# A three-stage block on one core: column-tiled bias products, transposing DMAs for integers and a written order in the first stage

## Chip, core and metric

The kernel runs on one core of a Trainium2 chip. Its time is the device time in microseconds (us), from launch to end. A core has TensorE (PE, matrix products from SBUF into PSUM), VectorE (DVE), ScalarE (ACT), GpSimd (POOL) and SyncE (SP), which here only issues DMAs. Each engine runs its own list of instructions in order, and the engines wait for each other through semaphores. PSUM has eight banks of 128 x 512 f32.

## The reference

Two batches of 2048 tokens with 512 channels, x, go through

```
c = clip(x * styles) @ W_cond.T, scaled per channel, plus a bias      # "cond"
h = rms_norm(c) ; r, i, f, g = h @ four matrices                       # "rec"
hs = scan(a(r), sqrt(1 - a*a) * sigmoid(i) * f) * gelu(g) + c
h2 = rms_norm(hs) ; x2 = x + hs + (gelu(h2 @ Wg) * (h2 @ Wf)) @ Wo     # "up", "down"
n  = norm(x2)
b  = norm(n * pw_g[id] + pw_b[id]) * cp_g[c] + cp_b[c]                 # the branch
cat = [w0*b, w1*(n*tm_g[c] + tm_b[c]), w2*(x2+vm), w3*(x2+vn), w4*(x2+vr), w5*(n*ms_g[m] + ms_b[m])]
o  = norm(silu(cat @ int_W1 + b1) @ int_W2 + b2)
out = x2 + int8(o) @ int8(rhs) * scales
```

vm, vn and vr are vectors per batch; c and m are small classes (5 and 3), id is one of 500. int8 rounds each token by its own largest value to the range -127 to 127.

## The kernel before, in words

Tokens lie on the free axis, channels on partitions, until the last stage. All large products are f32 and are done by a scheme of seven products in place of eight: `paired` (L138) and `paired_in_place` (L174) take the four quarters of the operand and of the weight, and run seven steps, each for two halves u of the output. After given steps (`at`, `then`, keyed by step or by step and u) other pieces of work are called in. DVE makes the sums of operand quarters, POOL those of the weights (`combine`, L119).

- The first stage, `cond` (L526), runs four stretches s of 1024 tokens. ACT copies a partial product out of PSUM with scale and bias (`tap`, L559), DVE adds the rest (`put`, L580) and clips, SP stores y_d. For the norm, four squares (ACT) are added up (DVE), summed over channels on PE, and turned into an inverse root (`inv_rms`, L446), which is stored in DRAM as r_d by four DMAs on ACT's queue (`store`, L478). In the stretches s = 0 and 3 the order on PE, DVE and ACT is that of the program (`ordered`, L279); in s = 1 and 2 a scheduler chooses it.
- `recur` (L682), `up` (L744) and `down` (L858) follow. The last call of `down` also prepares the last stage: `vectors` (L1157) multiplies three state vectors with three blocks of int_W1; `vectors_and_x` (L1197) adds those blocks, and loads the second half of the weight w_int.
- The last stage takes eight blocks of 512 tokens. `by_tokens` (L1321) turns x2 to tokens on partitions by PE transposes, norms, gathers the rows of pw by POOL's indirect DMA and norms again. `by_channels` (L1371) turns norm and branch back by PE. `gains` (L1378) multiplies by the class gains: a bf16 product with one-hot rows, four row groups side by side, then a DVE multiply. `up` (L1399) is the product with w_int, its operands x2T, lnT (the norm with the ms gains), tT (with the tm gains) and hT (the branch). `down2` (L1456) is the product with int_W2. The int8 part of block i-1 runs in `up` of block i: `last_norm` after step 0, `int8_product` (L1510) after step 2, with PE transposes of the integers (L1521), a DVE eviction with the lower clip (L1523) and the product with rq (`by_rhs`, L1488). The last block has its own, finer end (`part_norm`, `part_product`).
- Ahead of block 0 the biases of the classes are multiplied with w_int (L1568 to L1591) into a table of ten rows, which POOL splits into three bf16 parts for the product at L1429. PSUM there: two tiles of two banks for transposes and gains, used in turn, and four banks for products.

Edits of the diff touch `paired_in_place`, `store`, `cond`, `vectors`, `quarters`' callers, `stats`, `rstd_of`, `gather`, `by_channels`, `gains`, `up`, `int8_product` and the code that drives the last stage (L1564 on).

## Time and profile before

| | |
|---|---|
| three timed runs, us | 2039.68, 2043.04, 2043.53 (median 2043.04) |
| the profiled execution, us | 2037.24, span 2035.5 |
| granted PE clock, mean | 0.997 |
| first stage, 0 to 117 us | PE busy 110.5 |
| rec, 117 to 504 | PE busy 387.0 |
| up, 504 to 1090 | PE busy 584.7 |
| down, 1090 to 1395 | PE busy 303.8 |
| block 0 and its biases, 1395 to 1486 | PE busy 91.0, DVE 59.1 |
| blocks 1 to 7 up to the end's start, 1486 to 1978 | PE busy 491.2, DVE 374.2 |
| the end, 1978 to 2036 | PE busy 48.0 |
| all DMA | 193.5 MB, 95 GB/s over the span |

The table gives busy time by stage. A line of the timeline has the start and length in us, the engine and source line, the operation, the output and its inputs, shapes, and a count; brackets hold the idle time ahead of it and who ended it. An f32 matmul shows as two records. "ACTq" and "SPq" are the queues in which those engines issue DMAs. A line of the waits has who waited for whom, and the total, the number of times and the longest of these waits in us.

### The profile page before, as it was taken

Reading aid. Unit: us, or ns where it says so; the run is one execution under the profiler, and the core shown is the slowest. Engines: PE = TensorE matmul, PEld = TensorE weight load, DVE = VectorE, ACT = ScalarE, POOL = GpSimd, SP = SyncE. Lnnn points to the kernel's source line nnn. Section 1 sums busy time; section 2 is a strip of 40 time slices with the busy share of each in tenths; the row PEclk is TensorE's granted clock in tenths of the full one; section 3 lists DMA queues with packets and bytes.
Section 4 is the critical chain, followed back from the end, with each engine's and each line's share of the span. In section 5 each row is a group of like instructions: output and inputs, shape, how many; then the busy total and the mean of one; then the engine's idle time right before and its main releaser. Section 6 shows DMA issues by size and latency. Waiting matters only on the chain.

```text
span 2035.5 us, 17108 instructions
## 1 busy us (share of the span) xinstructions
PE 2016.1 (99%) x6404; PEld 1073.6 (53%) x6412; DVE 1188.6 (58%) x1804; ACT 652.4 (32%) x861; POOL 155.1 (8%) x126
## 2 busy tenths in 40 slices
PE   9899999999999999999999999999999999999998
PEld 5344444444444444444444444435777777777774
DVE  6757666666534224334226375486587687688675
ACT  4457777777422222222220000001302302302301
POOL 0332000000400000000010000072000000000000
PEclk9999999999999999999999999999999999999998
DMA  6571223121412112111334765624101101111000
GB/s 214 183 215 52 83 64 96 48 93 63 152 44 92 43 42 93 42 41 64 114 117 158 259 208 199 227 88 166 54 29 63 72 33 63 65 39 62 22 21 21
DMA packets 84547, 193.54 MB, mean 95 GB/s; under 512 B 6608, under 2 KB 34806, under 8 KB 80368
## 3 DMA queue, kind: packets, MB, share of 16 engines
q1 hardware_dynamic: 79792, 175.64, 25.5%
q0 software_dynamic: 4608, 16.78, 2.5%
q8 instruction: 50, 0.82, 0.2%
q14 instruction: 33, 0.27, 0.0%
q10 hardware_dynamic: 64, 0.03, 0.0%
HBM read 133.27 MB, written 58.75 MB: 94 GB/s over the span
## 4 chain that ended last, share of the span: by engine, by line
PE 96%; DVE 2%; DMA 1%; ACT 1%; issue 0%; ACTq 0%; SPq 0%; DVEq 0%
PE up_a L132 16%; PE ps_h_a L132 11%; PE rec_a L132 11%; PE up_d L132 8%; PE dn_a L132 7%; PE ps_h_d L132 6%; PE rec_d L132 5%; PE ps_o L1467 5%; PE up_b L132 4%; PE dn_d L132 4%; PE ps_h_b L132 3%; PE rec_b L132 3%; PE y_a L132 2%; PE dn_b L132 2%; PE ps_f L1491 1%; PE y_d L132 1%
## 5 line engine op out<-in xcount | busy, mean ns | idle before, releaser
L132 PE MATMUL up_a<-h,w_up 128*128 128x512 f32 x384 | 172.6, 592 | 0.0
L132 PE MATMUL dn_a<-op,w_dn 128*128 128x512 f32 x384 | 167.4, 594 | 0.0
L773 DVE SCALAR_TENSOR_TENSOR prod<-up_d,cols,k 128x512 f32<-128x512 f32 x48 | 35.9, 750 | 201.2 <-ACT k L265 201.2
L265 ACT COPY k<-up_a 128x512 f32<-128x512 f32 x144 | 83.9, 584 | 198.2 <-PE up_a L132 194.2
L753 ACT ACTIVATE gate<-gate,cols 128x512 f32<-128x512 f32 x96 | 68.8, 721 | 215.4 <-DVE gate L752 214.3
L132 PE MATMUL up_a<-h2T,w_up 128*128 128x512 f32 x288 | 129.5, 592 | 0.0
L132 PEld LDWEIGHTS up_a<-h,w_up 128*128 128x128 f32 x384 | 73.1, 190 | 91.7 <-issue 89.3
L132 PEld LDWEIGHTS dn_a<-op,w_dn 128*128 128x128 f32 x384 | 72.3, 190 | 88.6 <-issue 86.1
L132 PE MATMUL rec_a<-h,w_rec 128*128 128x512 f32 x256 | 115.1, 592 | 0.0
L132 PE MATMUL rec_a<-hT,w_rec 128*128 128x512 f32 x256 | 115.1, 592 | 0.0
L1467 PE MATMUL ps_o<-int_w,h 128*128 128x512 f32 x224 | 103.6, 606 | 0.0
L132 PEld LDWEIGHTS up_a<-h2T,w_up 128*128 128x128 f32 x288 | 54.8, 190 | 68.8 <-issue 68.8
L132 PE MATMUL up_b<-h,w_up 128*128 128x512 f32 x192 | 86.3, 592 | 0.0
L132 PE MATMUL up_d<-h,w_up 128*128 128x512 f32 x192 | 86.3, 592 | 0.0
L132 PE MATMUL dn_d<-op,w_dn 128*128 128x512 f32 x192 | 84.2, 595 | 0.0
L132 PEld LDWEIGHTS rec_a<-h,w_rec 128*128 128x128 f32 x256 | 48.7, 190 | 61.1 <-issue 60.9
L132 PEld LDWEIGHTS rec_a<-hT,w_rec 128*128 128x128 f32 x256 | 48.7, 190 | 61.1 <-issue 60.7
L265 ACT COPY k<-rec_a 128x512 f32<-128x512 f32 x96 | 55.4, 579 | 67.3 <-PE rec_a L132 65.8
L752 DVE TENSOR_TENSOR gate<-up_b,k 128x512 f32<-128x512 f32 x48 | 32.9, 690 | 71.7 <-PE up_b L132 70.6
L132 PE MATMUL up_d<-h2T,w_up 128*128 128x512 f32 x144 | 65.2, 592 | 0.0
L1467 PEld LDWEIGHTS ps_o<-int_w,h 128*128 128x128 f32 x224 | 40.3, 190 | 46.5 <-issue 46.5
L132 PE MATMUL ps_h_a<-tT,w_int 128*128 128x256 f32 x256 | 64.3, 385 | 0.0
(394 smaller groups left out, 3474.6 us busy)
## 6 DMA issues: line engine op xcount, KB each, us to landing
pp_d<-prod SPq DMA_DIRECT2D x48, 512.0 KB
op<-pp_d SPq DMA_DIRECT2D x16, 1536.0 KB
y_d<-y SPq DMA_DIRECT2D x16, 512.0 KB
h<-y_d SPq DMA_DIRECT2D x4, 2048.0 KB
yr<-y_d SPq DMA_DIRECT2D x16, 512.0 KB
hs_d<-yr SPq DMA_DIRECT2D x16, 512.0 KB
h<-hs_d SPq DMA_DIRECT2D x4, 2048.0 KB
op<-in_xT SPq DMA_DIRECT2D x32, 256.0 KB
```

The lines of the kernel that those rows point to most:

```text
L132: ins = nc.tensor.matmul(ps, ws[k // 2][:, slot, k % 2, ts(u, P)], xs[k], start=(first and k == 0), stop=(last and k == n - 1), skip_group ...
L265: nc.scalar.copy(t, ps)
L752: nc.vector.tensor_add(gate[u][:, half], ps, kept)
L753: nc.scalar.activation(gate[u][:, half], gate[u][:, half], AF.Gelu, bias=col("L0_attn_mlp_gate_b", fs[u]),)
L773: nc.vector.scalar_tensor_tensor(prod[u][:, b_], ps, col("L0_attn_mlp_fc_b", fs[u]), kept, ALU.add, ALU.add)
L1467: nc.tensor.matmul(ps, h1[:, c, ts(j, P)], w2[:, c, :], start=(c == 0), stop=(c == C - 1))
L1491: nc.tensor.matmul(ps, qT[:, ts(c, P)], rq[:, c, :], start=(c == 0), stop=(c == C - 1))
```

## The change

Four edits come together.

1. First stage: all four stretches run in the order of the program. The operand sums of stretch s+1 are called in stretch s (the first at step 6, the second at its end, the other two at step 2 of s+1), and the squares of stretch s at steps 1 and 2 of s+1. The r_d stores of the very last inverse root go through SP.
2. `vectors` takes its twelve operands from one padded tile, filled by three copies; the loads and sums of the second half of w_int are called after step 3 of the last `down` and no longer after step 1.
3. The twelve products of the class biases are put in four column groups of 32, two accumulated and four not, and one product adds the groups up later. PE follows the program's order in the first block up to the end of step 1 of `up`; steps 0 and 1 are done in two halves of their operands each, with gains and branch transposes between. In block 0 tT holds the ms gains and lnT the tm gains, and x's second transposes are queued one half step earlier.
4. The integers are clipped on DVE ahead of the transpose, which is now a DMA on SP from SBUF to SBUF, one for each pair of 128 tokens. The product of the first pair stays behind step 2, that of the second goes behind the first half of step 3. The last block keeps its PE transposes.

```diff
     def paired_in_place(ws, B11, B21, B12, B22, banks, tap, out11, out12, out21, out22,
-                        then=(), added=None, shared=False):
+                        then=(), added=None, shared=False, late=None):
...
             X = [x[:, k, :] for x in X for k in range(x.shape[1])]
-            for u in U:
-                ins = product(ps[u], ws, slot, X, u, first and not (u and shared), last)
-                if (step.n, u) in then:
-                    then[step.n, u]()
+            if late and step.n < 2:
+                n = len(ws) // 2
+                for h in (0, 1):
+                    for u in U:
+                        ins = product(
+                            ps[u], ws[n * h : n * h + n], slot, X[2 * n * h : 2 * n * h + 2 * n], u,
+                            first and not h and not (u and shared), last and h,
+                        )
+                        if (step.n, u, h) in then:
+                            then[step.n, u, h]()
+                mids.append(ins)
+            else:
+                for u in U:
+                    ins = held["ins"] = product(
+                        ps[u], ws, slot, X, u, first and not (u and shared), last
+                    )
+                    if not u:
+                        mids.append(ins)
+                    if (step.n, u) in then:
+                        then[step.n, u]()
             ends.append(ins)
...
         step.n = 0
-        ends = []
+        ends, mids = [], []
...
         step(pa, 0, B11, True, False)
-        k1 = tap(1, pa, None)
+        with late(0) if late else nullcontext():
+            k1 = tap(1, pa, None)
         pb = banks("b")
-        sums(B11, B12, B11)
-        sums(B12, B22, B12)
-        step(pb, 1, B21, True, not added)
-        more(1, pb)
-        out11(pb, k1)
+        if late:
+            step(pb, 1, B21, True, not added)
+        with late(1) if late else nullcontext():
+            sums(B11, B12, B11)
+            sums(B12, B22, B12)
+        if not late:
+            step(pb, 1, B21, True, not added)
+        def c11():
+            more(1, pb)
+            out11(pb, k1)
+        if not late:
+            c11()
         pd = banks("d")
         step(pd, 6, B22, True, False)
+        if late:
+            c11()
         more(2, pd)
...
         out21(pa)
-        return ends
+        return ends, mids
...
+            queue = nc.sync if (m, s) == (2, NS - 1) else nc.scalar
             for j in range(4):
-                nc.scalar.dma_start(r_d[m, s][:, ts(j, n)], r[32 * j : 32 * j + 1])
+                queue.dma_start(r_d[m, s][:, ts(j, n)], r[32 * j : 32 * j + 1])
...
+    chain = {}
...
         b = s // PER_S
-        at = parts_of_rest((4, 0), *AT[1:])
+        at = merged(chain, parts_of_rest((4, 0), *AT[1:]))
         if s == 0:
...
         else:
-            xs = operands(load_x(s), f"xT_{s}")
+            xs, sums = ahead
+            at = merged(at, {(2, 1): sums[2:4]})
         y, late = {}, []
...
             ahead[:] = operand_sums(Bt, "hT_0")
-            at = merged(
-                at, {(2, 1): chunks[0:2], (3, 1): chunks[2:3], (5, 0): chunks[3:4], (6, 1): ahead[1][0:1]}
-            )
+            at = merged(at, {(2, 1): chunks[0:2], (3, 1): chunks[2:3], (5, 0): chunks[3:4]})
+        else:
+            ahead[:] = operand_sums(load_x(s + 1), f"xT_{s + 1}")
+        at = merged(at, {(6, 1): ahead[1][0:1]})
         paired([w_cond[b]], xs, f"y_{s}", tap, put(0, a_), put(0, b_), out21, put(2, b_), at)
-        if s == NS - 1:
-            ahead[1][1]()
-        tot = None
-        for o in (2, 3, 0, 1):
-            tot = squares(tot, y[o])
+        ahead[1][1]()
+        tot = []
+        def square(o):
+            tot.append(squares(tot.pop() if tot else None, y[o]))
+        chain.clear()
+        chain.update({
+            k: [lambda o=o: square(o)] for k, o in (((1, 0), 2), ((1, 1), 3), ((2, 0), 0), ((2, 1), 1))
+        })
         rest.append(inv_rms(tot, 1, s))
...
     for s in range(NS):
-        with ordered() if s in (0, NS - 1) else nullcontext():
+        with ordered():
             done = cond(s)
...
     idx_pw = w3.tile([P, NT], mybir.dt.int32, name="idx_pw", bufs=1)
-    betas = w3.tile([P, 3, C, R], FP, name="betas", bufs=1)
+    betas_flat = w3.tile([P, 3 * C * R + G - R], FP, name="betas", bufs=1)
+    betas = betas_flat[:, : 3 * C * R].rearrange("p (m c r) -> p m c r", c=C, r=R)
     dn = ph1.enter_context(ExitStack())
...
             for c in range(C):
-                lhsT = small.tile([P, G], FP, tag="vec", name=f"vec_{m}_{c}", bufs=4)
-                nc.vector.memset(lhsT, 0.0)
-                nc.vector.tensor_copy(lhsT[:, 8:10], vs[m][:, c, :])
                 nc.tensor.matmul(
-                    ps[G * c : G * c + G], lhsT, rhs(c), start=(m == 0), stop=(m == 2)
+                    ps[G * c : G * c + G], held["vec"][:, m, c, :], rhs(c),
+                    start=(m == 0), stop=(m == 2),
                 )
...
     def raw(k):
-        w = w8(f"int_w1_{k}")
-        nc.sync.dma_start(w, block_of(k))
+        w = w14(f"int_w1_{k}")
+        nc.sync.dma_start(w[:, 0:C], block_of(k))
         scaled(k, lambda c: w[:, c, :])
...
+    def vectors_as_operands(w):
+        v = padded(w, 3 * C).rearrange("p (m c) g -> p m c g", c=C)
+        for m in range(3):
+            nc.vector.tensor_copy(v[:, m, :, 8:10], vs[m])
+        held["vec"] = v
     w3_4 = [raw(3), raw(4)]
+    vectors_as_operands(w3_4[0])
     w_int, of_x = quarters(2, 1)
...
+    def second_weight():
         ws, _ = quarters(5, 0)
...
-    ends = down(NS - 1, {1: vectors_and_x, 2: hand_over})
+    ends, mids = down(NS - 1, {1: vectors_and_x, 2: hand_over, 3: second_weight})
     dn.close()
...
+    def norm_by_channels(i, k):
+        for q in PAIRS:
+            to_channels(block("lnT"), q, k["ln"][q], f"tr_l_{i}_{q}")
+    def branch_by_channels(i, k):
+        for q in PAIRS:
+            to_channels(block("hT", i), q, k["h0"][q], f"tr_h_{i}_{q}")
     def by_channels(i, k):
-        lnT, hT = k["lnT"], k["hT"] = block("lnT", i), block("hT", i)
-        for q in PAIRS:
-            to_channels(lnT, q, k["ln"][q], f"tr_l_{i}_{q}")
-        for q in PAIRS:
-            to_channels(hT, q, k["h0"][q], f"tr_h_{i}_{q}")
+        norm_by_channels(i, k)
+        branch_by_channels(i, k)
...
-        lnT, hT = k["lnT"], k["hT"]
-        if n == 0:
-            k["tT"] = block("tT")
-        dst, src = ((k["tT"], lnT), (lnT, lnT), (hT, hT))[n]
+        if n == 2:
+            dst = src = block("hT", i)
+        else:
+            src = block("lnT")
+            dst = block("tT") if n == (not i) else src
         ps = [tr(f"gain_{i}_{n}_{q}") for q in PAIRS]
...
         for q in PAIRS:
-            nc.vector.tensor_mul(duo(dst, q), ps[q], duo(src, q))
+            held["gained"] = nc.vector.tensor_mul(duo(dst, q), ps[q], duo(src, q))
...
         h_a, h_b = slice(0, H), slice(H, T)
-        first, second = (k["x2T"], k["lnT"]), (k["tT"], k["hT"])
+        tT, lnT = block("tT"), block("lnT")
+        masks, times = (lnT, tT) if i else (tT, lnT)
+        first, second = (k["x2T"], masks), (times, block("hT", i))
...
             w_int, *([t[:, :, h] for t in q] for h in (h_a, h_b) for q in (first, second)),
-            banks, tap, out11, out12, out21, out22, then, added, True,
+            banks, tap, out11, out12, out21, out22, then, added, True, None if i else behind_branch,
         )
...
-    def int8_product(i, qs, x2n):
-        for q in PAIRS:
-            t = o4s[i][q]
-            for j in (0, 1):
-                at = 2 * q + j
-                shifted(t[:, j, :], qs[:, 2, at : at + 1])
-            qn = place("q", 2, D, dtype=BF)
-            rounded(qn, t)
-            pt = tr(f"trq_{i}_{q}", BF)
-            for j in (0, 1):
-                for c in range(C):
-                    nc.tensor.transpose(pt[:, j, ts(c, P)], qn[:, j, ts(c, P)], identb)
-            qT = place("qT", 2, D, dtype=BF)
-            nc.vector.tensor_scalar(qT, pt, -127.0, None, ALU.max)
-            for j in (0, 1):
-                at = 2 * q + j
+    def int8_values(i, qs, q):
+        t = o4s[i][q]
+        for j in (0, 1):
+            at = 2 * q + j
+            shifted(t[:, j, :], qs[:, 2, at : at + 1])
+        qn = place(f"q{q}", 2, D, dtype=BF)
+        rounded(qn, t)
+        nc.vector.tensor_scalar(qn, qn, -127.0, None, ALU.max)
+        nc.sync.dma_start(
+            place(f"qT{q}", 2, D, dtype=BF).rearrange("p j (c t) -> p (j c) t", t=P),
+            qn.rearrange("p j d -> p (j d)"), transpose=True,
+        )
+    def int8_product(i, qs, x2n, q, behind):
+        t, qT = o4s[i][q], place(f"qT{q}", 2, D, dtype=BF)
+        for j in (0, 1):
+            at = 2 * q + j
+            with tc.issue_after(behind.ins):
                 by_rhs(t[:, j, :], qT[:, j, :], qs[:, 1, at : at + 1], f"ps_f_{i}_{q}_{j}")
-            nc.vector.tensor_add(t, t, duo(x2n, q))
-            nc.sync.dma_start(out_t[:, i * J + 2 * q : i * J + 2 * q + 2], t)
+        nc.vector.tensor_add(t, t, duo(x2n, q))
+        nc.sync.dma_start(out_t[:, i * J + 2 * q : i * J + 2 * q + 2], t)
...
         k = load(0)
-        normed_h = by_tokens(0, k, ends[4:])
-    pb = m2_ps.tile([P, D], FP, tag="mm", name="ps_bias")[:R]
-    pc = m2_ps.tile([P, D], FP, tag="mm", name="ps_bias_s")[:R]
-    n = 0
-    nc.tensor.matmul(pb, summing[:, 0:R], bias, start=True, stop=False)
+        normed_h = by_tokens(0, k, (ends[4], mids[5], ends[6]))
+        branch_stats = held["stats"]
+    first_block = ExitStack()
+    first_block.enter_context(tc.manual_schedule(engines={mybir.EngineType.PE}))
+    norm_by_channels(0, k)
+    pb = m2_ps.tile([P, D], FP, tag="mm", name="ps_bias")
+    pc = m2_ps.tile([P, D], FP, tag="mm", name="ps_bias_s")
+    def beta(m, c):
+        return betas_flat[:, (m * C + c) * R : (m * C + c) * R + G]
...
             nc.tensor.matmul(
-                pb, betas[:, m, c, :], w_int[at + c // 2][:, 1:4:2, c % 2, :],
-                start=False, stop=(n == 2 * C - 1),
-            )
-            n += 1
+                pb[G * c : G * c + G], beta(m, c), w_int[at + c // 2][:, 1:4:2, c % 2, :],
+                start=(m == 0), stop=(m == 2),
+            )
     for c in range(C):
         nc.tensor.matmul(
-            pc, betas[:, 1, c, :], w_int[2 + c // 2][:, 0:3:2, c % 2, :],
-            start=(c == 0), stop=(c == C - 1),
+            pc[G * c : G * c + G], beta(1, c), w_int[2 + c // 2][:, 0:3:2, c % 2, :],
+            start=True, stop=True,
         )
-    with tc.issue_after(normed_h.ins):
-        bias = bias[:R]
-        nc.vector.tensor_copy(bias, pb)
-        for k_ in (0, 1):
-            nc.vector.tensor_add(bias[:, ts(k_, 2 * P)], pc[:, 0 : 2 * P], bias[:, ts(k_, 2 * P)])
-        nc.vector.tensor_sub(bias[:, 2 * P :], bias[:, 2 * P :], pc[:, 2 * P :])
-        tables_done = split(3, bias, [place(f"tab{n % 2}", D, dtype=BF)[:R] for n in range(3)], nc.gpsimd)
-    by_channels(0, k)
-    for n in range(3):
-        gains(0, k, n)
+    def class_sums():
+        pcs = places["k1"]
+        nc.scalar.copy(pcs, pc)
+        lower, upper = slice(0, 2 * P), slice(2 * P, D)
+        with tc.issue_after(normed_h.ins):
+            nc.vector.tensor_add(bias, pb, bias)
+            for of in (lower, upper):
+                nc.vector.tensor_add(bias[:, of], bias[:, of], pcs[:, lower])
+            nc.vector.tensor_sub(bias[:, upper], bias[:, upper], pcs[:, upper])
+    def class_bias():
+        ps = m2_ps.tile([P, D], FP, tag="mm", name="ps_bias_sum")[:R]
+        nc.tensor.matmul(ps, summing[:, 0:R], bias, start=True, stop=True)
+        t = bias[:R]
+        nc.scalar.copy(t, ps)
+        tab = place("q1", 2, D, dtype=BF)
+        return split(3, t, [tab[:R, n % 2, :] for n in range(3)], nc.gpsimd)
+    with tc.issue_after(branch_stats.ins):
+        gains(0, k, 1)
+    def times():
+        with tc.issue_after(normed_h.ins):
+            gains(0, k, 0)
+    def behind_branch(n):
+        return tc.issue_after(held["gained"].ins if n else held["root"].ins)
+    tables_done = []
+    in_first = {
+        (0, 1, 0): steps(times, class_sums),
+        (0, 1, 1): lambda: branch_by_channels(0, k),
+        (1, 0, 0): lambda: gains(0, k, 2),
+        (1, 1, 0): lambda: tables_done.append(class_bias()),
+        1: first_block.close,
+    }
     last = None
...
         nxt = load(i + 1) if i + 1 < NB else None
-        then = {}
+        then = {} if last else in_first
         if last:
...
             then[0] = lambda: qs.append(last_norm(i - 1))
-            then[2] = lambda: int8_product(i - 1, qs[0], last["x2n"])
+            then[1] = lambda: [int8_values(i - 1, qs[0], q) for q in PAIRS]
+            then[2] = lambda: int8_product(i - 1, qs[0], last["x2n"], 0, held["ins"])
+            then[3, 0] = lambda: int8_product(i - 1, qs[0], last["x2n"], 1, held["ins"])
         if nxt:
```

More of the change, by code (lines that the diff above doesn't have):

```diff
@@ L106, in adaln_attn_ffn @@
     mm_ps = act.enter_context(tc.tile_pool(name="mm_ps", bufs=8, space=PSUM))
+    held = {}
     def mm(name):
@@ L457, in total @@
                 nc.tensor.matmul(
-                    ps[32 * j : 32 * j + 32], ones[:, 0:32], tot[:, ts(j, n)],
+                    ps[32 * j : 32 * j + 32], ones[:, 0:32], tot[0][:, ts(j, n)],
                     start=True, stop=True,
@@ L626, in load_rec @@
         w_rec.append(w)
-    chain = {}
     def links(s, o, r, i, f, g, last, new, tots):
@@ L673, in total @@
             if o == C - 1:
-                rest.append(inv_rms(tots.pop(), 2, s))
+                rest.append(inv_rms([tots.pop()], 2, s))
         gates()
@@ L850, in w14 @@
         return part(w3.tile([P, 7, 2, 2 * P], FP, tag="w", name=name), 7, D)
-    def w8(name):
-        return w14(name)[:, 0:C]
     def tmp(name):
@@ L912, in mm @@
         return sm_ps.tile([P, T], FP, tag="s", name=name)
-    held = {}
     def padded(w, n):
@@ L1080, in load_classes @@
         t = held["cls"] = w14("classes")
-        nc.vector.memset(betas, 0.0)
+        nc.vector.memset(betas_flat, 0.0)
         nc.vector.memset(t[:R, 0:3, :], 0.0)
@@ L1246, in place @@
         return t
-    carve(weight("zone_A", "A"), ("x2T0", 8), ("o4_0", 4), ("q", 2))
+    carve(weight("zone_A", "A"), ("x2T0", 8), ("o4_0", 4), ("q0", 2))
     carve(weight("zone_C", "C"), ("x2n0", 8), ("o4_1", 4), ("oh0", 1), ("oh1", 1))
@@ L1273, in stats @@
         nc.vector.bn_stats(st, t)
-        nc.vector.bn_aggr(mv[:, j, :], st)
+        held["stats"] = nc.vector.bn_aggr(mv[:, j, :], st)
     def rstd_of(mv, name):
@@ L1280, in rstd_of @@
         nc.vector.tensor_scalar(v[:, 0, :], mv[:, :, 1], 1e-5, None, ALU.add)
-        nc.scalar.activation(r, v[:, 0, :], AF.Sqrt)
+        held["root"] = nc.scalar.activation(r, v[:, 0, :], AF.Sqrt)
         nc.vector.reciprocal(r, r)
@@ L1314, in gather @@
     def gather(t, g):
-        with tc.issue_after(tables_done.ins) if J <= t < 2 * J else nullcontext():
+        with tc.issue_after(tables_done[0].ins) if J <= t < 2 * J else nullcontext():
             nc.gpsimd.indirect_dma_start(
```

## The prediction, made before the changed kernel ran

> **What bounds the kernel now.** I read the busy row first, then the waits of PE, then PE in order of time around each edit, then the queue that PE waits for.
>
> ```profile
> PE 2016.1 (99%) x6404; PEld 1073.6 (53%) x6412; DVE 1188.6 (58%) x1804; ACT 652.4 (32%) x861; POOL 155.1 (8%) x126
> ```
> ```profile
> PE y_a L132 <- ACT k L562: 5.1, 2, 2.7
> PE up_a L132 <- ACT k L265: 1.3, 1, 1.3
> PE ps_vec L1166 <- DVE vec L1165: 0.9, 2, 0.7
> ```
>
> PE works 2016.1 of 2035.5 us, and PE holds 96% of the chain of waits. So time can come from two places only: records taken off PE, and the few waits of PE (total, times, longest). The granted clock is 0.997 over the run, so no cheaper record is to be expected.
>
> **A, the first stage (L526-610).** Both y_a waits fall in the stretches s = 1 and 2, whose order a scheduler chose. The queue of ACT shows why:
>
> ```profile
> 57.77 0.71 ACTq L481 DMA_DIRECT2D r_d<-rms  x2
> 58.52 0.78 ACT L562 ACTIVATE k<-y_a,cols,dcoef 128x512 f32<-128x512 f32 x1 [4.46 <-DVE y L582]
> ```
>
> The copy k that frees PE's bank for the next product stands behind two stores of r_d, and these wait for DVE's three steps on rms (L474-476). PE stood still 2.67 us at 59.35 and 2.46 at 86.88. The change writes the order for all four stretches: the stores come behind the two out21 activations. Queued behind them on ACT are the next stretch's copy and four squares; that is the order of s = 3, in which PE never waits, so I take the 5.1 us as gone. DVE's sums for stretch s+1 move to (6,1) of stretch s, where DVE can be blocked by the 2 MB load of x. It is issued at 37.06 and 65.18 and needed some 20 us later; the r load with an h load of 2 MB ahead (92.92 to 104.81) took 11.9. Cover: about 8 us. The stores of the last rms move from ACT to SP, which takes away the up_a wait of the same kind at 547.99: 1.3 us. On SP they hold back only stores of pp_d. **A: 6.4 us.**
>
> **B, the vector products (L1157-1169).** PE in order of time:
>
> ```profile
> 1333.33 1.07 PE L1166 MATMUL ps_vec<-w_int,vec 128*32 128x512 f32 x8
> 1334.33 1.12 PE L132 MATMUL dn_d<-op,w_dn 128*128 128x512 f32 x2
> 1336.18 2.27 PE L1166 MATMUL ps_vec<-int_w,vec 128*32 128x512 f32 x6 [0.73 <-DVE vec L1165]
> 1338.62 1.05 PE L1166 MATMUL ps_vec<-int_w,vec 128*32 128x512 f32 x2 [0.17 <-DVE vec L1164]
> 1339.60 1.12 PE L132 MATMUL dn_d<-op,w_dn 128*128 128x512 f32 x2
> 1340.66 1.46 PE L1166 MATMUL ps_vec<-int_w,vec 128*32 128x512 f32 x6
> 1342.29 1.04 PE L1166 MATMUL ps_vec<-int_w,vec 128*32 128x512 f32 x2 [0.18 <-DVE vec L1165]
> 1343.27 9.28 PE L132 MATMUL dn_d<-op,w_dn 128*128 128x512 f32 x21
> ```
>
> A full-width f32 matmul is two records at 0.43 us spacing (8 in 3.43). Eight records in four column groups of 32 take 1.00 us (first line to second). 24 such records should cost 3.0, but the stretch is 9.94 us long, less four dn_d records (1.72): 8.2. The operands trickle in one by one from DVE (12 memsets, 12 copies, four buffers). After, three copies made long before fill one padded tile; the built order has all 12 matmuls in a row. Taking 2.8 (6 x 0.43 and some 0.2 for the changes of shape): **B: 5.4 us.** The second weight's loads and sums keep their places on SP, DVE and POOL, so moving its call costs nothing; it was done at 1372.9, 24 us before the bias products.
>
> **C, the bias products and the first block.**
>
> ```profile
> 1395.92 1.03 PE L1571 MATMUL ps_bias<-bias,sums 128*10 128x512 f32 x2
> 1396.79 7.03 PE L1574 MATMUL ps_bias<-w_int,betas 128*10 128x512 f32 x16
> 1403.65 3.60 PE L1580 MATMUL ps_bias_s<-w_int,betas 128*10 128x512 f32 x8
> 1407.18 0.66 PE L1296 MATMUL tr_l<-ident,zone_A 128*128 128x128 f32 x4
> ```
>
> 26 records one after another: 11.26 us. After: 24 in column groups (2.8) and one full matmul that adds the groups up (0.87), so 7.6 less. Here a rule is weighed against a row: the Trainium skill, "TensorE: Matmul & The Clock Gate", rules for kernel authors, gives small-M column groups 2.38x for three tiles of 32. At that rate 24 records (10.3 us) would take 4.3 and B and C would lose 1.5 each; the row above shows 3.4x with four, and I go by it.
>
> But these 11 us also hid the branch norm on DVE: its last normed tile is written at 1404.6, when PE was still at ps_bias_s. The change therefore reorders the block. Laying the built order on the old durations from 1395.0 (end of the down stage): one-hots 0.3, norm transposes 1.7, biases 2.8, gain 0.6, x2T halves 3.45, to 1404.0. DVE: the pw gather starts when the last reader of zone B is through, now 0.87 later (the x transposes are put between the halves of that step), so the branch statistics end at 1401.9, the first gained operand at 1404.2, the branch at 1407.1, the second gained operand at 1409.4. PE waits 0.3 at the second gain and 0.4 at the branch transposes, where a bank is still read, and next to nothing at hT (1415.0 against 1415.3). The table of biases (ACT copy, five POOL steps of 4.3 us, as from 1408.5 to 1412.9, then a small DMA) is ready near 1423 and asked for at 1425.7. Fewer switches from bf16 to f32, at 0.2 each: 0.6 won. At the end of block 0 the lnT copy must now wait for the last product, as the two operands have changed places: 0.65 lost. **C: 7.6 + 0.6 - 0.7 - 0.65 = 6.9 us.**
>
> **D, the integers, seven blocks.** PE loses two sets of eight transposes:
>
> ```profile
> 1507.00 0.61 PE L1521 MATMUL trq<-identb,zone_A 128*128 128x128 bf16 x8
> 1507.54 0.39 PE L1429 MATMUL ps_h_d<-zone_C,tables 30*128 30x256 bf16 x2
> ...
> 1510.55 0.61 PE L1521 MATMUL trq<-identb,zone_A 128*128 128x128 bf16 x8
> 1511.00 1.95 PE L132 MATMUL ps_h_d<-x2T,w_int 128*128 128x256 f32 x8
> ```
>
> 0.54 + 0.45 = 0.99 us, times 7 is **6.9 us**. DVE gives up two 0.68 us evictions and takes two clips of bf16, no dearer.
>
> The new thing is a DMA of 256 KB that transposes, and PE now waits for it. DVE's order after puts the first half's clip at about 1501.7, the second's at 1503.5; PE asks for them at 1507.0 (end of step 2) and 1512.5 (half of step 3). Window: 5.3 us, and 10.8 for both if they run one behind the other. SP has nothing else queued there: x2T was loaded at 1457.7, and out_y comes behind. If the first is late, all of PE behind it is late.
>
> No row shows a transposing DMA. Nearest row: the plain load of 512 KB at the start, issued at 1.18, used by PE at 5.02, 3.8 us. A gather of half a megabyte takes longer:
>
> ```profile
> pw<-in_pw,idx_pw POOLq DMA_INDIRECT x16, 5.4
> ```
>
> A rule speaks against this edit. "VectorE: DVE Perf Modes", The three transpose paths, gives 1309 ns for one 128x128 bf16 transpose by DMA against 390 on TensorE, and advises TensorE. PE's row says 0.06 per transpose, better still. Eight times 1.309 is an estimate of 10.5 us per DMA, against 3.8 by the row. With T for one DMA the stall of a block is about 2T - 10.8 where T is over 5.4: nothing at 3.8; 10.2 at 10.5, or 71 us in seven blocks. The 1.3 us must hold a start-up that eight tiles in one instruction share, so I take 4 us and no stall, and keep 71 us for the range's other side.
>
> **Sum.** 6.4 + 5.4 + 6.9 + 6.9 = 25.6 us. The profiled execution took 2037.24 (span 2035.5), so 2011.6 by it; the three timed runs have a median of 2043.04, 5.8 above. Measured like these: **2017.5 us**.
>
> **Rivals.**
> 1. The forced orders bring waits of their own: a static order on ACT and DVE that blocks on the x loads, and a first block in which DVE's chain is the bound. For: in C DVE and PE meet within half a microsecond three times. Against: s = 3 and the recurrence run in such an order without a wait. A's 5.1 and C go: 25.6 - 12.0 = 13.6, 2029.4.
> 2. The transposing DMA is somewhat late, T of 6 to 6.6 us: stall 1.2 to 2.4 in each block, 8 to 17 us, about 2030.
> 3. Slower: the transposing DMA bounds the last stage. Place: ps_f at the end of step 2 and in the middle of step 3. Price 2T - 10.8 per block; from T = 7.2 us it eats 3.66 per block, that is, all 25.6 us. At 10.5: 2043 - 25.6 + 71 = 2088.
> 4. The edit does not do what it says: column groups one after another would undo B and C in part; the 1.00 us row speaks against it.
>
> **Chances.** Forecast 0.62 (2011 to 2024 by itself), rival 1 0.12, rival 2 0.10, rival 3 0.15, rival 4 0.01. About 0.2%, 4 us, is what a measurement of this kernel can tell. A T near 7 would leave no change; I give that 0.05, from rivals 2 and 3. So faster 0.81, same 0.05, slower 0.14. The range goes from 2010 (all runs as low as the fastest shown, and B and C at their best) to 2034 (rivals 1 and 2); it leaves out most of rival 3.
>
> **What would show it.** A: no y_a wait on ACT, none of up_a at 548. B: ps_vec in one piece of about 2.8 us. C: 24 bias records in about 2.8 us, PE waits under 1.5 us between there and block 1. D: no trq before the last block, ps_f of block 1 without a wait on a DMA. Wrong if PE waits for qT each block, or if a wait on DVE or a gained operand of over 3 us stands in the first block.

## The result and the profile after

The changed kernel takes 2020.4 us (median of six runs, 2016.54 to 2021.65) against 2043.28 for the kernel before (six runs, 2037.42 to 2047.88): ratio 0.9885, 95% interval 0.9865 to 0.9905. That is 22.9 us by the medians. The profiled execution of after took 2021.65 us with a span of 2019.9, so the two spans differ by 15.6 only. The trace of after comes from one of its longer runs and that of before, with a granted clock of 0.997, from one of its shorter: of 43 further runs of before the 17 at 0.997 took 2038.4 us in the mean and the ten at 0.995 took 2045.2.

The trace is cut at records that both kernels have: the first y_b, the first rec_a, up_a, dn_a, the first tr_oh (end of the down stage), the first product of block 1 and the end of the span. Lengths in us:

| | launch to y_b | first stage | rec | up | down | biases and block 0 | blocks 1 to 7, end |
|---|---|---|---|---|---|---|---|
| before | 16.18 | 100.75 | 387.60 | 579.16 | 311.31 | 90.76 | 549.74 |
| after | 18.68 | 95.08 | 387.60 | 577.57 | 313.47 | 83.20 | 544.3 |
| gained | -2.50 | 5.67 | 0 | 1.59 | **-2.16** | 7.56 | 5.44 |
| forecast | 0 | 5.1 | 0 | 1.3 | **5.4** | 6.9 | 6.9 |

The first column is no part of the change. The product ps_styles, whose code is the same in both kernels, took 1.92 us in before and 3.54 in after, and over the profiled executions told of below in which this stretch has the code of after the first y_b lies between 15.07 and 18.68. What is left is 18.1 us. One step stands out: the down stage became longer where 5.4 us were forecast as a gain.

The busy row of after, and the top of its waits of PE (total, times, longest):

```profile
PE 2001.7 (99%) x6292; PEld 1067.4 (53%) x6300; DVE 1174.8 (58%) x1783; ACT 653.4 (32%) x863; POOL 153.8 (8%) x127
```
```profile
PE dn_a L134 <- DVE op L222: 5.3, 1, 5.3
```

Both y_a waits and the up_a wait are gone; a new one of 5.3 us stands on top. PE in order of time shows where:

```profile
1328.43 1.06 PE L1203 MATMUL ps_vec<-w_int,int_w 128*32 128x512 f32 x8
...
1331.14 20.87 PE L134 MATMUL dn_d<-op,w_dn 128*128 128x512 f32 x48
1357.33 12.79 PE L134 MATMUL dn_a<-op,w_dn 128*128 128x512 f32 x24 [5.32 <-DVE op L222]
```

From 1328.43 to 1331.14 the vector products take 2.71 us in one piece, as forecast. But 21 us later PE stands 5.32 us for an operand sum of DVE, and the 24 records after it take 12.79 us where the same 24 took 10.46 before: 2.33 us more. 5.4 - 5.3 - 2.3 is the -2.2 of the table. The other engines of after in the same stretch (the kernel's lines: 1246 adds blocks of int_W1 on POOL, 1223 loads the second weight, 1195 scales it, 222 is the operand sum of the down product):

```profile
1329.56 10.35 POOL L1246 TENSOR_TENSOR w_int<-w_int,int_w 128x512 f32<-128x512 f32 x8 [140.95 <-PE ps_vec L1203]
1335.05 7.31 SPq L1223 DMA_DIRECT2D w_int<-in_int_W  x8
1338.77 2.84 DVE L1195 TENSOR_SCALAR w_int<-w_int,wsm 128x512 f32<-128x512 f32 x2 [6.79 <-POOL w_int L1246]
...
1347.24 5.70 DVE L1195 TENSOR_SCALAR w_int<-w_int,wsm 128x512 f32<-128x512 f32 x4
1352.86 4.41 DVE L222 TENSOR_TENSOR op<-op,op 128x3072 f32<-128x3072 f32 x1
```

Read from the bottom: the sum B22 - B11, which step 4 of the last `down` multiplies, stands on DVE behind eight scaling steps. These wait for the load, and the load waits until POOL has read the tile that it overwrites. The same chain in the kernel before ended here:

```profile
1357.61 4.42 DVE L201 TENSOR_TENSOR op<-op,op 128x3072 f32<-128x3072 f32 x1
1362.26 10.46 PE L132 MATMUL dn_a<-op,w_dn 128*128 128x512 f32 x24
```

The sum was written at 1362.03 and read at 1362.26. The chain had 0.2 us to spare, and since PE came just behind it, no view of before listed a wait.

The records of the biases, and the longer wait of the first block, in after:

```profile
1394.63 1.93 PE L1643 MATMUL ps_bias<-w_int,betas 128*32 128x512 f32 x16
1396.37 1.04 PE L1648 MATMUL ps_bias_s<-w_int,betas 128*32 128x512 f32 x8
...
1402.94 0.39 PE L1442 MATMUL gain<-zone_C,tables 30*128 30x512 bf16 x2 [0.81 <-DVE tT L1447]
```

24 records in 2.72 us (1394.63 to 1397.35), one product more of 0.96 (ps_bias_sum, L1665), and with a shorter wait of 0.34 ahead of this one 1.15 us of waits. And block 1: the first integer product, and the two portions of x transposes, of which one stands between the two integer products:

```profile
1496.83 1.89 PE L1548 MATMUL ps_f<-rq,qT 128*128 128x512 bf16 x7
...
1498.97 0.87 PE L1383 MATMUL tr_x<-ident,zone_A 128*128 128x128 f32 x6
...
1508.51 1.25 PE L1383 MATMUL tr_x<-ident,zone_A 128*128 128x128 f32 x10
```

No bracket with a wait: PE does not stand for the transposing DMA, here or in a later block.

### The profile page after: what moved, and what is told of

It is laid out like the page before. It is cut to its first block, busy times and chain, and to the rows that moved or that the text cites. A ratio compares the mean times of both kernels' runs of the same rounds, so it can differ in the third digit from the quotient of the medians.

```text
span 2019.9 us, 16905 instructions
## 1 busy us (share of the span) xinstructions
PE 2001.7 (99%) x6292; PEld 1067.4 (53%) x6300; DVE 1174.8 (58%) x1783; ACT 653.4 (32%) x863; POOL 153.8 (8%) x127
## 4 chain that ended last, share of the span: by engine, by line
PE 95%; DVE 1%; issue 1%; POOL 1%; DMA 1%; ACT 0%; SPq 0%; POOLq 0%; ACTq 0%; DVEq 0%
PE up_a L134 16%; PE ps_h_a L134 11%; PE rec_a L134 11%; PE up_d L134 8%; PE dn_a L134 7%; PE ps_h_d L134 6%; PE rec_d L134 5%; PE ps_o L1524 5%; PE up_b L134 4%; PE dn_d L134 3%; PE ps_h_b L134 3%; PE y_a L134 3%; PE rec_b L134 3%; PE dn_b L134 2%; PE y_d L134 1%; PE ps_f L1548 1%
## 5 line engine op out<-in xcount | busy, mean ns | idle before, releaser
L222 DVE TENSOR_TENSOR op<-op,op 128x3072 f32<-128x3072 f32 x16 | 55.8, 3486 | 12.3 <-PE dn_d L134 6.5
```

Of the source, the lines that this page charges most:

```text
L222: nc.vector.tensor_sub(t, p, q)
```

## Experiments

The question was first where B went, then whether A, C and D come from the steps that the prediction names. Two theories of B: (1) the chain POOL, load, scaling, sum had no slack before, and PE's gain ran into it; (2) the moved call `second_weight`, or something else, made the sum late.

**1. B alone, on the kernel before.** The padded vector tile only; the second weight is called where it was.

```
-                lhsT = small.tile([P, G], FP, tag="vec", name=f"vec_{m}_{c}", bufs=4)
-                nc.vector.memset(lhsT, 0.0)
-                nc.vector.tensor_copy(lhsT[:, 8:10], vs[m][:, c, :])
-                nc.tensor.matmul(ps[G * c : G * c + G], lhsT, rhs(c), ...)
+                nc.tensor.matmul(ps[G * c : G * c + G], held["vec"][:, m, c, :], rhs(c), ...)
```

> The kernel before with part B alone: one padded tile of vector operands, 12 products in a row; the call that loads the second weight keeps its old place. My prediction's term B: PE gains 5.4 us, time about 2037.5 against 2043. Theory 1 (the chain POOL sums, weight load, DVE scaling, operand sum ends at a fixed 28.8 us after step 1 of the last down product, and had no slack before): the vector products shrink from 8.2 to 2.8 us, PE then waits some 5.3 us for the operand sum, the records after it are some 2 us slower: time the same or up to 2.3 us longer, 2043 to 2045. If the moved call was to blame for the late sum, there is no wait here and the time is 2037.5.

Measured: 2041.05 us against 2042.26, ratio 1.0001 (0.9989 to 1.0014). PE at step 4 of the last down product:

```profile
1362.86 12.53 PE L132 MATMUL dn_a<-op,w_dn 128*128 128x512 f32 x24 [5.19 <-DVE op L201]
```

The same wait and the same slow records, without the moved call; the down stage takes 313.05 us, 1.74 more than before. Part B alone is worth nothing, and moving the call is not to blame. (The medians hardly differ, although this trace also has a first stage of 102.44 us, 1.69 longer than before with the same code; the last section says why.)

**2. The sum ahead of the scaling.** One edit on the kernel after: the loads and scaling steps of the second weight are issued behind the sum.

```
-                nc.vector.tensor_sub(t, p, q)
+                held["summed"] = nc.vector.tensor_sub(t, p, q)
...
-        ws, _ = quarters(5, 0)
+        with tc.issue_after(held["summed"].ins):
+            ws, _ = quarters(5, 0)
```

> The kernel after, with the four scaling steps of the second weight put behind the operand sum B22-B11 on DVE. Theory 1 (my account of part B): in the kernel after, PE stands 5.3 us for that sum, which is queued on DVE behind scaling steps that wait for POOL and then for a load; the 24 records after that wait take 12.8 us instead of the 10.5 of before. With the sum ahead, the wait goes and the slow records with it: PE is 7 to 8 us shorter in the down stage, the time about 2013 us against 2020 for the kernel after, the bias products still find their weight in time (it is then complete near 1373 to 1378, asked for near 1390). Theory 2: the sum is late for another reason (its own operand, or DVE's work ahead of the scaling): the wait stays at 5 us, whoever ends it, and the time stays at 2020. Theory 3: the scaling steps now come late, and PE waits for the second weight at the bias products, so that what goes in the down stage comes back there: time within 2 us of 2020.

Measured: **2010.89 us** (2009.3 to 2014.01), ratio to before 0.9852 (0.9834 to 0.9870). The sum now comes first on DVE, at 1338.88, ahead of the scaling at 1342.60, and waits only for PE to be through with its operand. DVE and PE in order of time:

```profile
1338.88 3.79 DVE L222 TENSOR_TENSOR op<-op,op 128x3072 f32<-128x3072 f32 x1 [2.99 <-PE dn_d L134]
```
```profile
1348.98 10.46 PE L134 MATMUL dn_a<-op,w_dn 128*128 128x512 f32 x24
```

The down stage takes 305.87 us: 7.60 less than after, and 5.44 less than before, which is the prediction's 5.4. The second weight is complete in time for the biases, where PE does not wait. This version beats both kernels.

**3. The slow records.** Idle matmuls between steps 3 and 4 keep PE at work where it stood; the sum stays late. 22 of them, and then 6.

```
+        with tc.issue_after(held["ins"].ins):
+            fill = tr_A[0].tile([P, 2, D], FP, tag="tr", name="fill")
+            for _ in range(22):
+                nc.tensor.matmul(fill[:, 0, 0:P], ones, ones, start=True, stop=True)
         ws, _ = quarters(5, 0)
```

> The kernel after, with 22 idle matmuls of 128x128 put on PE between steps 3 and 4 of the last down product, where PE stood 5.3 us for DVE. They fill the stand and do nothing else; their product is not used. If the 24 records after the stand are slow (12.8 us instead of 10.5) because PE had been idle, they run at 10.3 to 10.6 here, the granted clock does not dip there, and the time falls by about 2.3 us against the kernel after (2018). If they are slow for another reason (DVE or DMA traffic that stands beside them), they still take 12 to 13 us and the time is that of the kernel after or up to 0.5 us over it, 2020 to 2021.

> As the kernel with 22 idle matmuls in the gap of the last down product, but with 6 of them: PE works 1.4 us on and then stands some 3.9 us, in place of 0.3 (22 of them) and 5.3 (none). If the slow records after the gap come from the length of PE's stand and there is a threshold between the 2.7 us that left no trace in the first stage and 5.3 us, this run says on which side 3.9 lies: the 24 records take 10.5 us (below) or 12.5 to 12.8 (above). If the loss grows with the length, some 11 to 12 us. In all cases the time is between 2018 and 2021.

Measured: 2019.16 us with 22 (2015.98 to 2019.97), 2020.79 with 6 (one run). By the medians the 22 bring 1.2 us, by the traces the forecast 2.3: the down stage takes 311.16 us in place of 313.47. PE behind the fillers, which end at 1356.9 with 22 and 1353.4 with 6; first 22, then 6:

```profile
1357.22 10.57 PE L134 MATMUL dn_a<-op,w_dn 128*128 128x512 f32 x24 [0.28 <-DVE op L222]
```
```profile
1357.40 12.26 PE L134 MATMUL dn_a<-op,w_dn 128*128 128x512 f32 x24 [3.99 <-DVE op L222]
```

With PE at work the 24 records take 10.57 us although they start at the same time as in after, so DMA and DVE beside them are not the cause. With 6 fillers the loss is 1.8 us, a size that the expectation did not name; the last section gives the reason. The granted clock by stretches, for after (window, length, PE busy with count, granted clock, DMA share and rate):

```profile
1354.00:1356.00 2.00, 0.00 (x0) 0.75 0.00 0
1356.00:1357.00 1.00, 0.00 (x0) 0.50 0.00 0
...
1361.00:1362.00 1.00, 1.00 (x3) 0.58 0.44 180
```

PE fell idle at 1352.0. 3.0 us later the clock halved, and it stayed at 0.50 for 6.8 us (half of 1354 to 1356, up to 0.84 of 1361 to 1362), of which 4.5 were work: worth 2.3 us. With 22 fillers it stays at 1.00 throughout. The Trainium skill, "TensorE: Matmul & The Clock Gate", section Why this matters for your kernels, tells authors to leave no idle gap of PE over about 3 us; the stands of 5.3 and 4.0 us here agree, and the rows add what such a gap costs, but experiment 5 shows that a shorter one can cost too.

**4. The integers on PE again.** The kernel after with `int8_product` of before (transposes and evictions; no DMA).

```
-        nc.sync.dma_start(place(f"qT{q}", ...), qn.rearrange("p j d -> p (j d)"), transpose=True)
...
+                    nc.tensor.transpose(pt[:, j, ts(c, P)], qn[:, j, ts(c, P)], identb)
+            nc.vector.tensor_scalar(qT, pt, -127.0, None, ALU.max)
```

> The kernel after with the integers of the last stage transposed on PE again, as before: two sets of eight transposes and two evictions in each block, no transposing DMA. By the traces of the two kernels the last seven blocks and the tail took 544.3 us with the DMA and 549.7 without: theory: 5 to 6 us longer than the kernel after, 2025.5 to 2026. By the prediction's term (0.99 a block) 6.9: 2027.3. If the gain of the last stage came from elsewhere (the order of the first block's operands), less than 3: 2020 to 2023.

Measured: 2024.5 us (2024.31 to 2025.09); the last column of the table becomes 549.92. The DMA is worth 5.6 us by the trace (0.80 a block) and 4.1 by the medians, less than the 6.9 forecast.

**5. How long the transposing DMA takes.** PE asks right behind step 1.

```
-            then[1] = lambda: [int8_values(i - 1, qs[0], q) for q in PAIRS]
-            then[2] = lambda: int8_product(i - 1, qs[0], last["x2n"], 0, held["ins"])
-            then[3, 0] = lambda: int8_product(i - 1, qs[0], last["x2n"], 1, held["ins"])
+            then[1] = lambda: [int8_values(...) for q in PAIRS] + [int8_product(..., q, ...) for q in PAIRS]
```

> A measurement of the transposing DMA: the kernel after with both integer products of each block put directly behind step 1, so that PE stands until the first half of the integers has landed, and then, if the second is later than its 1.7 us of product, until that has landed. PE should ask near 1491.4, 0.2 us after the first DMA is issued (1491.2); the second is issued 1.5 us later. By the prediction's T = 4: a wait of 3.8 in each block, 27 us in seven, time near 2047, and hardly a wait at the second product (landing 1.5 us later if both run side by side). At T = 5.6, the most that the trace of after allows: 5.4 a block, 38 us, 2058. If two such DMAs run one behind the other, the second product waits a further T less 1.7 us: 2.3 us a block more at T = 4.

Measured: 2045.8 us (one run), the last column 573.0. SP's queue and PE in block 2:

```profile
1566.89 1.24 SPq L1576 DMA_TRANSPOSE qT<-zone_A  x1
```
```profile
1570.14 3.63 PE L1548 MATMUL ps_f<-rq,qT 128*128 128x512 bf16 x15 [2.67 <-DMA qT<-zone_A]
```

From the issue (1.24 us of SP's time included) to PE's start: 3.25 us here, 3.13 to 3.62 over the seven blocks. In this block the second product follows without a break, so the second DMA, issued 1.5 us later, had landed some 3.5 us after its issue at most. Yet the two do not move data side by side: in windows of 0.1 us the DMA engines are busy from 1568.1 to 1569.4 (share 0.7 to 1.2), nearly idle to 1569.6, and busy again to 1570.9. So of the 3.25 us some 1.2 pass before the first data, 1.4 are the transfer and 0.7 the rest up to PE's start; issued 1.5 us apart, the two transfers just do not meet.

The waits add up to 3.0 us a block (21.2 in all), but the stage grew by 28.7. That the time came near the 2047 expected for T = 4 is luck: the waits were shorter, and the rest is the clock again. In the four blocks with a low clock the two products took 1.6 to 2.9 us longer than the 3.46 of the others. Stands of 2.90, 3.06, 4.67 and also one of 2.56 were followed by a granted clock of 0.50, three of 2.59, 2.67 and 2.73 were not. Block 1 and block 2 (windows as above):

```profile
1491.00:1494.00 3.00, 3.00 (x8) 0.50 0.00 0
...
1570.00:1574.00 4.00, 3.81 (x17) 1.00 0.26 48
```

**6. The biases full width.** The class-bias operands 128 columns wide, in one group (class biases differ from the reference's).

```
-                pb[G * c : G * c + G], beta(m, c), ..., start=(m == 0), stop=(m == 2),
+                pb, beta(m, c), ..., start=(m == 0 and c == 0), stop=(m == 2 and c == C - 1),
```

> The kernel after with the bias products 128 columns wide, one after another in one group, instead of in four column groups of 32 at a time; everything else of the first block as the change has it. The operands' further columns hold neighbouring vectors and unset memory, so the class biases that the last stage adds are not the reference's. By column groups: 24 records at 0.43 instead of 2.72 us in all, 7.6 us more on PE, less the 1.15 us of waits for the gained operands in the first block, which DVE no longer causes: 6.4 to 7.6 us over the kernel after, 2026.8 to 2028. If it was the order by halves that brought the gain of 7.6 us between the down stage and block 1, and DVE bounds the first block anyway: less than 3 us, 2020 to 2023.

Measured: 2025.79 us (2023.92 to 2027.83), 5.4 over after by the medians; by the trace the biases and block 0 take 89.66 us, 6.46 over after. The 24 records are 10.4 us long (1392.26 to 1402.66), the second wait at the gains shrinks from 0.81 to 0.30 and the first is gone:

```profile
1392.26 7.03 PE L1643 MATMUL ps_bias<-w_int,betas 128*128 128x512 f32 x16
...
1407.32 0.39 PE L1442 MATMUL gain<-zone_C,tables 30*128 30x512 bf16 x2 [0.30 <-DVE tT L1447]
```

So the column groups make the gain, and cost 0.85 us of it in waits that they lay bare.

**7. The order of the first stage.** First only the written order undone in the middle stretches, then all of part A (operand sums, squares and stores back at their old places too).

```
-        with ordered():
+        with ordered() if s in (0, NS - 1) else nullcontext():
             done = cond(s)
```

> The kernel after with the order of stretches s = 1 and 2 of the first stage left to the scheduler again; the first and the last stretch, and the stores of the last rms, stay as the change has them. Theory: the written order is what removed PE's two waits for the copy k on ACT; they come back, 5 us: from the first y_b to the recurrence 100 us instead of 95.1, time 2025.4. If the waits went for another reason (the squares, sums and stores that moved to other places), few or none of them come back: 2020 to 2022.

> The kernel after with all of part A undone: the order of stretches s = 1 and 2 left to the scheduler, operands, squares and sums where they were before, and the stores of the last rms on ACT's queue. Theory (prediction's A, with the size that the two traces give): two waits of PE for the copy k on ACT, 2.7 and 2.5 us, and one of 1.3 to 1.6 for up_a come back; y_b to the recurrence takes 100.75 us in place of 95.08, the next stage 579.2 to 579.4 in place of 577.57: 7.3 us over the kernel after, 2027.7. The run with the order alone undone brought 2.9 us in the trace, since there the squares and sums stood elsewhere. If A's gain were a matter of the execution and not of these edits, less than 4 us: below 2024.5.

Measured: 2024.05 us (2020.55 to 2027.34) for the order alone, first stage 98.01, 2.93 over after; 2028.68 (2024.43 to 2036.54) for all of A, first stage 100.75, up 579.37. The largest waits of PE in these stages, first with the order undone, then with all of A undone:

```profile
PE y_a L134 <- ACT k L601: 1.4, 1, 1.4
```
```profile
PE y_a L134 <- ACT k L600: 5.1, 2, 2.7
...
PE up_a L134 <- ACT k L297: 1.5, 1, 1.5
```

With all of A undone, both stages come back to the lengths of before, to 0.2 us. The order alone gives back only 2.9 of the 5.7: the first of its two expectations missed the size, since squares, sums and stores had moved as well and the scheduler arranged the rest differently. The two halves of A do not add up as separate edits, and no run here parts them further.

**8. The end filled.** In the kernel of experiment 2 the clock halved at 1998 us, in PE's 3.4 us wait of the last block, and stayed so to the end. 13 matmuls without a use are put there.

```
+        if j == 0:
+            fill = tr("fill")
+            for _ in range(13):
+                nc.tensor.matmul(fill[:, 0, 0:P], t[:, 0:P], t[:, 0:P], start=True, stop=True)
```

> The kernel with the sum ahead of the scaling steps (2010.9), and with 13 matmuls of one part of the last block, whose product is not used, on PE in its 3.4 us wait before the last but one integer product. In that kernel the granted clock halves at 1998 us, after 2.6 us in which PE had stood, and stays at 0.50 to the end: two products of four records take 1.89 us each. Theory (a stand of PE of some 3 us lowers the clock): with the wait filled the clock stays at 1.00 there, the two products take 1.0 us each and the transposes between them 0.4 in place of 0.6. The first lies beside DVE's work, the second and the transposes on the path to the end: about 1.0 us off the span, 2009.9. If the clock falls for another reason, it is 0.50 there again and the time is 2010.9 or some tenths over.

Measured: 2011.29 us (2010.97 to 2013.07): no gain that the runs can tell. The clock stays at 1.00 and the products shrink from 1.89 to 1.04, as expected:

```profile
2002.51 0.40 PE L1617 MATMUL trq<-identb,zone_B 128*128 128x128 bf16 x4 [1.46 <-DVE zone_B L1544]
2003.45 1.04 PE L1549 MATMUL ps_f<-rq,pw 128*128 128x512 bf16 x4 [0.54 <-DVE pw L1623]
```

But the last column only falls from 544.34 to 543.8. DVE is the bound there: in its built order the eviction of the first product now comes ahead of the rounding that the next transposes read, and PE waits 1.46 us for them. The expectation left out that DVE's order can change with the edit.

## Why the prediction was right, and where it was wrong

**Direction and size.** Faster, 2020.4 against 2017.5, inside the range. None of the four rivals came true; one step failed and another was too large. That the median came within 2.9 us of the forecast is in part luck: B is missing with 7.5 us, and the medians hold 4.8 us more than the 18.1 of the traces, from differences between executions that the forecast did not count.

**A held.** 6.4 forecast, 7.26 measured (5.67 + 1.59). The waits went as said (5.1 of the 5.67); no new one came from the x loads. Experiment 7 shows that the edits of A made it. Which link held the copy k is less sure than the prediction says: its own line names DVE's y (L582), which ended at 58.40, just ahead of the stores' issue at 58.48, and no run parts the two.

**B failed, at the sentence "The second weight's loads and sums keep their places on SP, DVE and POOL, so moving its call costs nothing".** The 5.4 us on PE were sized right, and the moved call does cost nothing (experiment 1). What was missed is that work which keeps its place behind the vector products does not become faster with them. It was weighed against the distant reader (the bias products, 24 us later), not against the near one: the scaling steps stand on DVE in front of an operand sum that the running product asks for. From the end of step 1 to the end of that sum 28.6 us passed in before and 28.8 in after. PE came for it 28.9 us after step 1 in before, and 23.5 in after. So all 5.4 us came back as a wait, and a loss of clock of 2.3 on top. A mere look at what DVE did at 1357 to 1362 in the trace of before would have shown it. The chain is also so long because DVE and POOL slow each other there (last section).

**C held**: 6.9 forecast, 7.56 measured. Products: 7.6 forecast, 11.26 - 2.72 - 0.96 = 7.58 measured. 24 records that cost 0.43 each one after another (10.3) in 2.72 are a gain of 3.8x; the rule's 2.38x (on that page it stands under Why this matters for your kernels) was rightly set aside, the row of 3.4x was still low. Waits at the gains: 1.15 instead of 0.3; the wait at the branch transposes did not come. The end of block 0, counted at -0.65, and the switches, at +0.6, made up some 1.1 together, which no run here parts; so the sum is nearer than two of its terms.

**D held in kind and was too large**: 0.99 a block forecast, 0.78 measured. Nothing waits for the DMA: T is 3.3 us against the 4 taken, of which the transfer is 1.4. The estimate of 10.5 from the 1309 ns per tile of the Trainium skill ("VectorE: DVE Perf Modes", The three transpose paths) does not hold for a DMA of eight tiles in one instruction; rival 3 had no ground, and the page's advice of TensorE (it stands there under Rules for kernel authors) was rightly not followed here. The missing 0.2 is a mis-sized term: the transposes had been counted at their full 0.99 with nothing in their place. In after, the sixteen x transposes no longer run in one piece but as 6 and 10: 0.80 + 1.09 us by their starts instead of 1.74 before, so 0.15 of it goes back into one more change of shape.

**The sum.** 7.26 - 2.16 + 7.56 + 5.44 = 18.1 us against 25.6; the 7.5 missing are B's. With that chain repaired (experiment 2) the medians give 31.4 us (2042.26 - 2010.89).

## What to carry to other kernels

Before taking time out of one engine, follow every chain of other engines that starts with it and ends at its next waiting instruction: a chain that ended 0.2 us before its reader shows in no list of waits, and it keeps its length when the reader comes earlier. In a queue worked in order, put what the running product needs next ahead of a prefetch that itself waits for a load. Price a stand of PE higher than its length: here 5.3 us of standing cost 7.6, and in the seven traces with this stand (4.99 to 5.63 us) the records behind it lost a further 1.8 to 2.4 us.

## What the runs showed of the hardware that was not expected

- The low clock comes in whole portions of 3.41 us, on a fixed grid. In the kernel with 6 fillers it lasted from 1358.36 to 1361.78, in blocks 1 and 5 of experiment 5 from 1490.78 to 1494.20 and from 1808.22 to 1811.64: 3.42 us each (worked out from the mean clock of the windows around their ends). In after, and in blocks 4 and 7 of experiment 5, it lasted 6.8, twice as much. The four starts in experiment 5, columns as above:

```profile
1490.00:1491.00 1.00, 0.88 (x3) 0.89 0.70 130
1724.00:1727.00 3.00, 0.14 (x2) 0.88 0.88 130
1808.00:1809.00 1.00, 0.61 (x1) 0.61 1.11 207
1963.00:1967.00 4.00, 0.13 (x1) 0.78 0.52 99
```

A mean of 0.89 over 1 us is 0.22 us at half rate, so the low clock starts at 1490.78 there, and in the other rows at 1726.28, 1808.22 and 1965.24. These lie 235.50, 81.94 and 157.02 us apart: 69, 24 and 46 times 3.413, to within 0.03 us. That is the free-running window of 3413 ns which the Trainium skill, "TensorE: Matmul & The Clock Gate", describes under What's actually happening.

- What counts is how much of one such window PE stands, not how long the stand is. Laid on this grid, the stands of over 1.2 us (launch and last block left out) of all twelve traces fall in two groups, worked out from PE's waits and the granted clock of each trace: 13 take up 2.17 us or more of one window, and the clock halves at the end of the first such window; 12 take up at most 1.95 us of any, and it does not. So a stand of 2.56 us (block 5 of experiment 5, 2.41 of it in one window) was followed by the low clock and one of 2.73 (block 6, split into 1.05 and 1.68) was not. In the first stage the same stand of 2.67 us left no trace in before, but in the trace of experiment 1 the clock halved at 59.54, 1.2 us after PE was back at work, which cost 1.7 us. The same page has the half rate come after a whole idle window; here less was enough, and the measurement decides.
- DVE and POOL slow each other here. A scaling step of 128 x 512 took 0.48 us near 1200 in after, where POOL was idle, and up to 1.48 beside POOL's sums; the operand sum took 3.35 us at 1326.88 and 4.41 at 1352.86, and POOL's step beside the latter 4.37 in place of 1.26 to 1.44. The eight scaling steps and the sum of the late chain took 15.0 us; with POOL idle they would take 7.2, an estimate from these figures. How much of the 5.3 us wait this made is open, since the steps also waited for the load.
- A DMA that transposes 128 x 1024 bf16 (256 KB) from SBUF to SBUF holds SP for 1.23 to 1.36 us while it is issued, against 0.38 to 0.40 for the plain store of an output tile in the same stage.
- The first 19 us vary between executions: ps_styles took between 1.92 and 3.54 us. The granted clock of that stretch in after stands at 1.00, so its cause stays open.
